# Where the lengths of the keys are computed in a second-order attention: on the transposed keys, or with tokens on partitions

## The chip, the core and the metric

The kernel runs on one core of one Trainium2 chip. A core has five engines with an instruction queue each: TensorE (PE in the profile; PEld is its loader of weights), VectorE (DVE), ScalarE (ACT), GpSimd (POOL) and SyncE (SP), and 16 DMA engines. Each queue is worked off in order, and an instruction starts when the semaphores that it waits for have been reached. The metric is the time of one execution on the device in microseconds, as the median of the runs shown.

## What is computed

The program is a graph network of two layers for 3125 nodes, 256 channels and 100,000 edges. Each layer adds to `x` a graph attention over the edges, a "mix" attention over all nodes, and a feed-forward part. The change touches the mix of layer 1, which has 8 heads of 32 channels (`N` = 3125, `scale` = 32 to the power 1/4):

```python
def _normalize(t):
    n = jnp.linalg.norm(t, axis=-1, keepdims=True)
    return t / jnp.maximum(n, EPS)
...
v1 = jnp.concatenate([jnp.ones((B, H, N, 1), dtype=v.dtype), v], axis=-1)
qn = _normalize(q) * (scale * temperature)
kn = _normalize(k) * scale
vN = v1 / N
kv_mod = jnp.einsum('bhni,bhnj,bhne->bhije', kn, kn, vN)
kv = jnp.einsum('bhnd,bhne->bhde', kn, vN)
vsum = jnp.sum(vN, axis=-2)[:, :, None, :]
y = A * jnp.einsum('bhni,bhnj,bhije->bhne', qn, qn, kv_mod) + scale ** 2 * Bc * jnp.einsum('bhnd,bhde->bhne', qn, kv) + scale ** 4 * Cc * vsum
```

So each key is divided by its length over the 32 channels of its head and multiplied by `scale`; then sums over all tokens of products of two key channels and a value channel are needed, and sums of one key channel and a value channel.

## The kernel before, in words

**Layer 1.** Two recorded streams of work share the engines. The graph attention (`l1_gnn_slots`, `by_slots`) goes through 25 blocks of 128 nodes, in 63 steps of up to 16 edges per node. GpSimd gathers a row of keys and values for each edge slot (L635) into one of five `kv` buffers. TensorE turns the edge features (L2596), ScalarE copies them out (L2598), TensorE multiplies them by the weights (L2599) into one of two `e` buffers in PSUM, and VectorE adds them to the gathered rows (L2604). VectorE then multiplies by the query (L985), sums over the channels (L989), and weights and halves the values (L1014, L1020); TensorE adds up what is left (L1023), which frees `kv` for the next gathers.

**The mix beside it.** `l1_mix_pairs` is a Python generator. After each of the 63 steps, `Beside` takes about two of its units, so that its instructions are recorded between those of the graph attention. A scheduler then fixes the order on each engine; the order of recording sets priorities, not the order itself. For each half of the heads (`c` = 0, 1; four heads, 128 channels) there is a key pass over all tokens and then a query pass. The key pass goes by groups of 4 tiles of 125 tokens (6 groups of 500 tokens and one of 125).

**For a group** `unit_T` computes the transposed keys, channels on partitions and tokens along the free dimension: TensorE multiplies (L2879), ScalarE adds the bias into `x` (L2884) and squares it (L2888), TensorE sums the squares over each head's 32 partitions with the block-diagonal matrix of ones `k.bd`, which also spreads each sum over the 32 partitions (L2890), ScalarE takes the root (L2892), VectorE clamps it (L2893), takes the reciprocal (L2894) and multiplies `x` by it and by `scale` (L2895). All of these are 128 x 500. The query pass uses the same function.

**For a tile** of 125 tokens: TensorE computes the values (L2912) into bank 0 of the two-bank PSUM tile `w`, of which there is one buffer; VectorE sets a column of ones (L2920) and adds the bias (L2921); TensorE turns the keys (L2924) into bank 1; ScalarE copies them out (L2925) and squares them (L2926); TensorE adds the tile to the moments `mom` (L2927, L2930, L2933). For the products of two different channels, TensorE multiplies the transposed keys of each head by `sel`, which has two ones in each column, so that each column is a sum of two channels (L2944, two heads in the two banks of `w`); ScalarE squares both banks in one instruction (L2949); after two such rounds TensorE multiplies the squares by the values and adds to `pairs` (L2953). The constants `neg` and `selT` later take the squares of single channels off again.

Of the kernel before, what the change touches and what calls it, by code (L numbers as in the profile page):

```python
# [10 lines left out]
F32 = mybir.dt.float32  # L11
I32 = mybir.dt.int32
BF16 = mybir.dt.bfloat16
AF = mybir.ActivationFunctionType
ALU = mybir.AluOpType
# [4 lines left out]
P = 125  # L20
# [39 lines left out]
def load_w(k, pool, w, name):  # L60

    kk, m = w.shape
    t = pool.tile([128, kk // 128, m], F32, name=name, tag=name)
    k.nc.sync.dma_start(t, w.rearrange("(c p) m -> p c m", p=128))
    return t


def load_col(k, pool, b, name):

    m = b.shape[0]  # L70
    t = pool.tile([128, m // 128], F32, name=name, tag=name)
    k.nc.sync.dma_start(t, b.rearrange("(c p) -> p c", p=128))
    return t
# [217 lines left out]
def after(k, ins, others):  # L291

    for other in others:
        k.tc.add_manual_dep(
            ins.ins, other.ins.name,
            mybir.DependencyInfo(mybir.DependencyClass.Sync, mybir.DependencyReason.DATA),
            reason="rows of the table",
        )
# [2543 lines left out]
def l1_mix_pairs(k, tabs, a, pl):  # L2842
# [6 lines left out]
    nc, NT, N = k.nc, k.NT, k.N  # L2849
    s = 32.0 ** 0.25  # L2850
    one, wp, xp, sp, ip, pp, pa, pb = pl
    two = lambda: pp.tile([128, 2, 512], F32, name="w", tag="w")
    ps_tile = lambda: two()[:, 0]
    wqkv = load_w(k, one, a["Wqkv"], "wqkv")
    bcol = load_col(k, one, a["bqkv"], "bcol")
# [6 lines left out]
    for h in range(8):  # L2862
        r = slice(h % 4 * 32, h % 4 * 32 + 32)
# [5 lines left out]
    def load_cols(gi, ng):  # L2869
        xT = ip.tile([128, 2, 4 * P], F32, name="xTg", tag="xTg")  # L2870
        nc.sync.dma_start(xT[:, :, : ng * P], tabs.cols[gi, :, :, : ng * P])
        return xT

    def unit_T(xT, ch, ng, scale, factor):

        w_ = ng * P
        ps = ps_tile()
        for ci in range(2):
            nc.tensor.matmul(  # L2879
                ps[:, :w_], wqkv[:, ci, ch * 128 : ch * 128 + 128],  # L2880
                xT[:, ci, :w_], start=(ci == 0), stop=(ci == 1),
            )
        x = wp.tile([128, 4 * P], F32, name="x", tag="x")
        nc.scalar.activation(  # L2884
            x[:, :w_], ps[:, :w_], AF.Identity, bias=bcol[:, ch : ch + 1], scale=scale
        )
        sq = xp.tile([128, 4 * P], F32, name="xsq", tag="xsq")
        nc.scalar.activation(sq[:, :w_], x[:, :w_], AF.Square)  # L2888
        ps = ps_tile()
        nc.tensor.matmul(ps[:, :w_], k.bd, sq[:, :w_], start=True, stop=True)  # L2890
        r = xp.tile([128, 4 * P], F32, name="r", tag="r")
        nc.scalar.activation(r[:, :w_], ps[:, :w_], AF.Sqrt)  # L2892
        nc.vector.tensor_scalar_max(r[:, :w_], r[:, :w_], 1e-12)  # L2893
        nc.vector.reciprocal(r[:, :w_], r[:, :w_])  # L2894
        nc.vector.scalar_tensor_tensor(  # L2895
            x[:, :w_], x[:, :w_], factor, r[:, :w_], op0=ALU.mult, op1=ALU.mult
        )
        return x

    for c in range(2):  # L2900
        pairs = pa.tile([128, 512], F32, name="pairs", tag="pairs")
        mom = pb.tile([128, 512], F32, name="mom", tag="mom")
        for gi, (g0, ng) in enumerate(k.groups):
            xT = load_cols(gi, ng)
            kT = unit_T(xT, 2 + c, ng, 1.0, s)
            for j in range(ng):
                i = g0 + j
                first, last = i == 0, i == NT - 1
                tk = slice(j * P, j * P + P)
                ps = two()  # L2910
                for ci in range(2):
                    nc.tensor.matmul(  # L2912
                        ps[:P, 0, :128], xT[:, ci, tk],
                        wqkv[:, ci, 2 * D + c * 128 : 2 * D + c * 128 + 128],
                        start=(ci == 0), stop=(ci == 1),
                    )
                kv = wp.tile([P, 257], F32, name="kvt", tag="kvt")
                k2 = wp.tile([P, 128], F32, name="k2", tag="k2")
                v = kv[:, 128:256]
                nc.vector.memset(kv[:, 256:], 1.0)  # L2920
                nc.vector.tensor_tensor(  # L2921
                    v, ps[:P, 0, :128], bv[:, c * 128 : c * 128 + 128], op=ALU.add
                )
                nc.tensor.transpose(ps[:P, 1, :128], kT[:, tk], k.ident)  # L2924
                nc.scalar.copy(kv[:, :128], ps[:P, 1, :128])  # L2925
                nc.scalar.activation(k2, ps[:P, 1, :128], AF.Square)  # L2926
                m0 = nc.tensor.matmul(  # L2927
                    mom[:, :257], kv[:, :128], kv, start=first, stop=last, skip_group_check=True
                )
                m1 = nc.tensor.matmul(  # L2930
                    mom[:, 257:385], k2, v, start=False, stop=last, skip_group_check=True
                )
                m2 = nc.tensor.matmul(  # L2933
                    mom[:, 385:386], v, k.ones_col[:P], start=False, stop=last, skip_group_check=True
                )
                if first:
                    after(k, m1, [m0])
                    after(k, m2, [m0])
                sqs = []
                for h0 in (0, 2):  # L2940
                    ps = two()
                    for b in range(2):
                        rows = slice((h0 + b) * 32, (h0 + b) * 32 + 32)
                        nc.tensor.matmul(  # L2944
                            ps[:P, b, :496], kT[rows, tk], sel[rows], start=True, stop=True,
                            tile_position=((h0 + b) * 32, 0),
                        )
                    sq = sp.tile([128, 2, 4 * P], F32, name="sq", tag="sq")
                    nc.scalar.activation(sq[:P, :, :496], ps[:P, :, :496], AF.Square)  # L2949
                    sqs += [sq[:, 0], sq[:, 1]]  # L2950
                for h in range(4):
                    rows = slice(h * 32, h * 32 + 32)
                    nc.tensor.matmul(  # L2953
                        pairs[rows, :496], v[:, rows], sqs[h][:P, :496], start=first, stop=last,
                        skip_group_check=True, tile_position=(0, h * 32),
                    )
                yield
# [16 lines left out]
        for t in range(4):  # L2974
            f = min(128, 496 - t * 128)
            fs = slice(t * 128, t * 128 + f)
            ps = ps_tile()
# [8 lines left out]
        ps = ps_tile()  # L2986
# [10 lines left out]
        for h in range(4):  # L2997
# [3 lines left out]
                op0=ALU.mult, op1=ALU.subtract,  # L3001
            )
        for gi, (g0, ng) in enumerate(k.groups):
            w_ = ng * P
            qT = unit_T(load_cols(gi, ng), c, ng, s, temp[:, c : c + 1])
            x = ip.tile([P, 4, D], F32, name="xg4", tag="xg4")
# [3 lines left out]
            ps = ps_tile()  # L3010
# [5 lines left out]
            ps = ps_tile()  # L3016
# [13 lines left out]
            for t in range(4):  # L3030
                f = min(128, 496 - t * 128)
                sqs = []
                for h0 in (0, 2):
                    ps = two()
                    for b in range(2):
# [3 lines left out]
                            start=True, stop=True, tile_position=((h0 + b) * 32, 0),  # L3039
                        )  # L3040
                    sq = sp.tile([128, 2, 4 * P], F32, name="sq", tag="sq")
# [14 lines left out]
            for j in range(ng):  # L3056
                ps = ps_tile()
# [158 lines left out]
def layer1(k, dram, a, out, tabs, order, show):  # L3216
    sub = lambda pre: {s[len(pre) :]: v for s, v in a.items() if s.startswith(pre)}
    top = ExitStack()
    (wp,) = pools(k, top, [("d_w", 1)])
    weights = l1_ffn_weights(k, wp, sub("L1_ffn_"))  # L3220
    with ExitStack() as st:
        units = l1_mix_pairs(k, tabs, sub("L1_mix_"), l1_mix_pools(k, st))
        beside = Beside(units, 2 * k.NT + 12 * len(k.groups), sum(len(steps(n)) for n in SLOTS))
        gout, sent = l1_gnn_slots(k, dram, tabs, order, a["edge_attr_64"], sub("L1_gnn_"), beside)
        beside.rest()
    with top as st:
        xp, wp = pools(k, st, [("x3", 1), ("r_wk", 4)])
        x = xp.tile([P, k.NT, D], F32, name="x3")
        for g0, ng in k.groups:
            k.nc.sync.dma_start(x[:, g0 : g0 + ng], tok(tabs.x)[:, g0 : g0 + ng])  # L3230

        def bring(g0, ng):
            g = slice(g0, g0 + ng)
            part = wp.tile([P, 4, D], F32, name="part", tag="part")
            after(k, k.nc.sync.dma_start(part[:, :ng], tok(gout[0 : k.N, :])[:, g]), sent)
            k.nc.vector.tensor_tensor(x[:, g], x[:, g], part[:, :ng], op=ALU.add)

        l1_ffn(k, dram, x, sub("L1_ffn_"), out, weights, bring)
# [111 lines left out]
```

## Time and profile before

| What | Value |
|---|---|
| Median of 3 runs | 5826.44 us (5819.25 to 5837.37) |
| The profiled execution | 5829.55 us, span 5827.8 us |
| TensorE busy (weight loads) | 4671.1 us, 80% of the span (2785.9) |
| VectorE busy | 4216.7 us, 72% |
| ScalarE busy | 1582.9 us, 27% |
| GpSimd busy | 2901.4 us, 50% |
| Layer 1's graph attention (first and last L2599) | 3504.6 to 5555.4 us |
| L2884, one of 500 tokens | 677 ns |
| L2921, one of 125 x 128 | 283 ns |
| L2925, L2926 | 266 and 283 ns |
| L2944, idle time of the squares' engine behind it | 186.0 us, 97 times |

"Busy" is the time in which an engine worked on an instruction. A busy TensorE is not TensorE at its peak, as matmuls overlap and its clock is granted in parts. A row of a group reads: line, engine, operation, output and inputs, shapes, count, then busy us and mean ns of one, then the idle time of the engine just before these instructions and the instruction whose end released most of it. Each matmul of 32-bit numbers is two instructions in the trace. Some records of matmuls are missing, so that counts can be below those of the program. The mean of one is from one profiled execution, that of the table.

### The profile page before, as it was taken

What the parts mean: (1) busy time and instruction counts of PE and PEld (TensorE: products, weight loads), DVE (VectorE), ACT (ScalarE), POOL (GpSimd) and SP (SyncE); (2) the same over time, 40 slices, a digit from 0 to 9 for tenths busy, and PEclk for the clock granted to TensorE, in tenths of its full rate; (3) what the DMA queues carried; (4) which work ended last, traced back from release to release, by engine and by line L of the source; (5) the groups of instructions that cost most, each with busy time, mean ns of one, the idle gap of its engine ahead of it and who ended that gap; (6) DMA issues with size and microseconds to landing.
All of it is one profiled execution on the core that took longest, in us unless ns stands there. A gap on an engine that the chain in (4) does not pass through costs nothing. (4 is left out here: it accounts for less than half of the span.)

```text
span 5827.8 us, 50130 instructions
## 1 busy us (share of the span) xinstructions
PE 4671.1 (80%) x16621; PEld 2785.9 (48%) x16621; DVE 4216.7 (72%) x6090; ACT 1582.9 (27%) x3284; POOL 2901.4 (50%) x2945
## 2 busy tenths in 40 slices
PE   3467997799957998789858857789888888888778
PEld 1245775566535676556545523334333434333335
DVE  5188888888578888988631256668787778878847
ACT  1033233233323334333411102222222222222221
POOL 2475775577366775667541035344444444444411
PEclk8778998799978999899859977888898789989979
DMA  5266776677466776667454355444453444545410
GB/s 152 61 197 187 217 198 187 182 210 207 146 178 192 208 207 188 198 195 208 147 164 137 109 167 173 121 124 129 137 148 119 132 124 139 150 131 150 137 59 23
DMA packets 374285, 908.58 MB, mean 156 GB/s; under 512 B 94268, under 2 KB 170074, under 8 KB 373892
## 3 DMA queue, kind: packets, MB, share of 16 engines
q0 software_dynamic: 232624, 725.48, 43.1%
q1 hardware_dynamic: 137412, 168.23, 8.9%
q10 hardware_dynamic: 3982, 11.59, 0.5%
q8 instruction: 134, 2.20, 0.2%
q14 instruction: 133, 1.09, 0.1%
HBM read 813.62 MB, written 91.30 MB: 155 GB/s over the span
## 5 line engine op out<-in xcount | busy, mean ns | idle before, releaser
L635 POOL DMA_INDIRECT kv<-kvtab,slots x2499 | 2425.6, 971 | 1742.1 <-PE acc L1023 691.6
L1170 PE MATMUL cps<-kv,ident 128*128 128x256 f32 x2644 | 688.8, 415 | 64.4 <-DVE kv L1154 63.1
L2604 DVE TENSOR_TENSOR kv<-kv,e 128x1024 f32<-128x1024 f32 (+1 forms) x448 | 503.4, 1137 | 252.1 <-PE e L2599 226.1
L1170 PEld LDWEIGHTS cps<-kv,ident 128*128 128x128 f32 x2644 | 548.9, 211 | 214.3 <-DVE kv L1154 82.4
L2599 PE MATMUL e<-weT,eaT 128*128 128x512 f32 (+1 forms) x896 | 516.6, 673 | 66.4 <-ACT eaT L2598 64.7
L1114 DVE TENSOR_TENSOR kv<-kv,qa 128x1792 f32<-128x1792 f32 (+2 forms) x230 | 478.6, 2081 | 98.4 <-DMA kv<-kvtab,slots 85.5
L1117 DVE TENSOR_REDUCE al<-kv 128x28 f32<-128x1792 f32 (+2 forms) x230 | 479.4, 2084 | 7.9
L1154 DVE TENSOR_TENSOR kv<-kv,qa 128x1792 f32<-128x1792 f32 (+2 forms) x230 | 475.3, 2074 | 0.0
L1857 PE MATMUL mm<-hTm,w 128*128 128x500 f32 (+1 forms) x896 | 364.4, 551 | 30.5 <-DVE xcur L1883 21.7
L1875 PE MATMUL mm<-w,hid 128*125 128x256 f32 x1600 | 378.5, 385 | 1.8 <-ACT hid L1865 1.8
L1023 PE MATMUL acc<-kv,ident 128*128 128x256 f32 x896 | 268.3, 463 | 76.9 <-DVE kv L1020 72.0
L1875 PEld LDWEIGHTS mm<-w,hid 128*125 128x125 f32 x1600 | 296.4, 190 | 65.2 <-issue 19.6
L2599 PEld LDWEIGHTS e<-weT,eaT 128*128 128x128 f32 (+1 forms) x896 | 153.7, 207 | 286.9 <-ACT eaT L2598 146.9
L1023 PEld LDWEIGHTS acc<-kv,ident 128*128 128x128 f32 x896 | 206.7, 237 | 165.8 <-DVE kv L1020 107.9
L1857 PEld LDWEIGHTS mm<-hTm,w 128*128 128x128 f32 x896 | 162.3, 196 | 177.5 <-issue 130.9
L989 DVE TENSOR_REDUCE al<-kv 128x56 f32<-128x1792 f32 (+2 forms) x115 | 238.7, 2075 | 4.6 <-issue 3.7
L985 DVE TENSOR_TENSOR kv<-kv,qa 128x1792 f32<-128x1792 f32 (+2 forms) x115 | 238.8, 2077 | 1.3
L1014 DVE TENSOR_TENSOR kv<-kv,al 128x1792 f32<-128x1792 f32 (+2 forms) x115 | 235.0, 2080 | 0.0
L2598 ACT COPY eaT<-e 128x128 f32<-128x128 f32 (+1 forms) x448 | 109.5, 267 | 411.7 <-PE e L2596 411.2
L1547 PE MATMUL mm<-ident,xh 125*128 125x125 f32 x400 | 96.7, 336 | 136.3 <-ACT xh L1537 128.0
L140 PE MATMUL mm<-wqv,hTm 128*125 128x512 f32 x400 | 187.5, 607 | 7.4 <-DMA wqv<-in_L_mix_Wv_dram 6.3
L1865 ACT ACTIVATE hid<-mm,b 128x500 f32<-128x500 f32 (+1 forms) x224 | 133.8, 632 | 198.3 <-PE mm L1857 196.8
(414 smaller groups left out, 7693.1 us busy)
## 6 DMA issues: line engine op xcount, KB each, us to landing
kv<-kvtab,slots POOLq DMA_INDIRECT x2499, 3.7
w<-in_L_ffn_w_dram SPq DMA_DIRECT2D x32, 512.0 KB
qd<-qT SPq DMA_DIRECT2D x24, 500.0 KB
kvtab<-st SPq DMA_DIRECT2D x12, 1000.0 KB
qT<-qd SPq DMA_DIRECT2D x24, 500.0 KB
xTg<-xcols SPq DMA_DIRECT2D x24, 500.0 KB
w<-in_L_mix_W_dram SPq DMA_DIRECT2D x8, 1024.0 KB
xs<-zero SPq DMA_DIRECT2D x16, 512.0 KB
```

Of the source, the lines that this page charges most:

```text
L635: return k.nc.gpsimd.indirect_dma_start(out=out, out_offset=None, in_=table, in_offset=bass.IndirectOffsetOnAxis(ap=index, axis=0),)
L985: nc.vector.tensor_tensor(kv[:, :m, :D], kv[:, :m, :D], q.unsqueeze(1).to_broadcast([128, m, D]), op=ALU.mult,)
L989: nc.vector.tensor_reduce(al[:, b0 : b0 + m], hv(kv[:, :m, :D]), axis=AX.X, op=ALU.add)
L1023: nc.tensor.matmul(acc[:, :D], k.ident, kv[:, j, D:], start=(b0 + j == 0), stop=(kv is bufs[-1][2] and j == left[-1]),)
L1114: nc.vector.tensor_tensor(kv[:, :m, :D], kv[:, :m, :D], q.unsqueeze(1).to_broadcast([128, m, D]), op=ALU.mult)
L1117: nc.vector.tensor_reduce(t["al"][:, b0 : b0 + m], self.heads(kv[:, :m, :D]), axis=AX.X, op=ALU.add)
L1154: nc.vector.tensor_tensor(v, v, t["w"][:, b0 : b0 + m].unsqueeze(3).to_broadcast([128, m, H, D // H]), op=ALU.mult)
L1170: self.k.nc.tensor.matmul(t["acc"][:, :D], self.k.ident, kv[:, j, D:], start=(b0 + j == 0), stop=(b == len(t["subs"]) - 1 and j == left[-1]),)
L1857: nc.tensor.matmul(ps[:, :w_], W["w1"][:, c, j * 128 : j * 128 + 128], o["hT"][:, c, :w_], start=(c == 0), stop=(c == 1),)
L1875: nc.tensor.matmul(ps[:P, :D], s["hid"][:, c, j * P : j * P + P], W["w2"][:, c, :], start=(c == 0), stop=False,)
L2599: nc.tensor.matmul(e[:, :n].rearrange("p b d -> p (b d)"), eaT[r], weT[r, :n].rearrange("p b d -> p (b d)"), start=True, stop=True,)
L2604: nc.vector.tensor_tensor(t, t, e[:, :n].unsqueeze(2).to_broadcast([128, n, 2, D]), op=ALU.add)
```

## The change

For the keys, `unit_T` is replaced by a new function. It stops after the squares: `x` stays as it is, without its length. The squares of a tile of 125 tokens become the stationary operand, and four columns of `k.bd` the moving one, so that the sums come out with tokens on partitions and one column for each head: 125 x 4 for a tile, 125 x 16 for a group. Root, clamp and reciprocal work on these. The factor is then put on in two places: VectorE multiplies the turned keys by it as it copies them out of PSUM, in place of ScalarE's copy, and ScalarE takes it as the scale operand when it squares the sums of two channels, one head in each instruction. The square `k2` is taken from the scaled keys in SBUF. The queries keep `unit_T`.

```diff
+    head0 = k.bd.rearrange("p (h d) -> p h d", d=32)[:, :, 0]
+
+    def keys_T(xT, ch, ng):
+
+        w_ = ng * P
+        ps = ps_tile()
+        for ci in range(2):
+            nc.tensor.matmul(
+                ps[:, :w_], wqkv[:, ci, ch * 128 : ch * 128 + 128],
+                xT[:, ci, :w_], start=(ci == 0), stop=(ci == 1),
+            )
+        x = wp.tile([128, 4 * P], F32, name="x", tag="x")
+        nc.scalar.activation(
+            x[:, :w_], ps[:, :w_], AF.Identity, bias=bcol[:, ch : ch + 1], scale=1.0
+        )
+        sq = xp.tile([128, 4 * P], F32, name="xsq", tag="xsq")
+        nc.scalar.activation(sq[:, :w_], x[:, :w_], AF.Square)
+        ps = ps_tile()
+        for j in range(ng):
+            nc.tensor.matmul(
+                ps[:P, j * 4 : j * 4 + 4], sq[:, j * P : j * P + P], head0, start=True, stop=True
+            )
+        r = wp.tile([P, 16], F32, name="r4", tag="r4")
+        nc.scalar.activation(r[:, : ng * 4], ps[:P, : ng * 4], AF.Sqrt)
+        nc.vector.tensor_scalar(
+            r[:, : ng * 4], r[:, : ng * 4], 1e-12, 1.0 / s, op0=ALU.max, op1=ALU.mult
+        )
+        nc.vector.reciprocal(r[:, : ng * 4], r[:, : ng * 4])
+        return x, r
...
-            kT = unit_T(xT, 2 + c, ng, 1.0, s)
+            kT, r4 = keys_T(xT, 2 + c, ng)
...
-                nc.scalar.copy(kv[:, :128], ps[:P, 1, :128])
-                nc.scalar.activation(k2, ps[:P, 1, :128], AF.Square)
+                rj = r4[:, j * 4 : j * 4 + 4]
+                nc.vector.tensor_tensor(
+                    kv[:, :128].rearrange("p (h d) -> p h d", d=32),
+                    ps[:P, 1, :128].rearrange("p (h d) -> p h d", d=32),
+                    rj.unsqueeze(2).to_broadcast([P, 4, 32]), op=ALU.mult,
+                )
+                nc.scalar.activation(k2, kv[:, :128], AF.Square)
...
-                    nc.scalar.activation(sq[:P, :, :496], ps[:P, :, :496], AF.Square)
+                    for b in range(2):
+                        nc.scalar.activation(
+                            sq[:P, b, :496], ps[:P, b, :496], AF.Square,
+                            scale=rj[:, h0 + b : h0 + b + 1],
+                        )
```

In the new kernel the lines that the prediction names are L2907 (was L2879, for the keys), L2919 (the lengths), L2951 (was L2921), L2954 (L2924), L2956 (the new multiplication), L2961 (L2926), L2962 (L2927), L2979 (L2944), L2985 (the squares, L2949) and L2992 (L2953).

## The prediction

> **What bounds the kernel now.** I read the page's totals first (TensorE is busy for 80% of the span, VectorE for 72%, and neither is full), then found the two stretches in which the changed code runs: the first and last instructions of the sum-of-pairs matmuls (L2953) and of the key pass's `x` (L2884) put the key pass of the first half of the heads at 3513 to 3995 us and that of the second at 4565 to 4991 us. The view of busy time by stretch gives for them:
>
> ```profile
> 3513.00:3995.00 482.00, 393.90 (x1271) 182.18 (x1271) 341.56 (x356) 119.98 (x266) 217.31 (x225) 0.84 0.46 133
> 4565.00:4991.00 426.00, 374.32 (x1253) 172.64 (x1253) 321.54 (x351) 121.15 (x264) 189.51 (x192) 0.87 0.44 129
> ```
>
> Columns: stretch, its length, busy us of TensorE, weight loads, VectorE, ScalarE, GpSimd, then granted clock, DMA share, GB/s. TensorE leaves 88 + 52 = 140 us idle in the two passes, VectorE 245, ScalarE 667. So TensorE is nearest to the bound, and the passes end when its stalls end. Next, what TensorE waited for: the groups of the two instructions that stand right behind the keys' normalisation. First the timeline at one normalisation:
>
> ```profile
> 3703.59 0.41 DVE L2893 TENSOR_SCALAR r<-r 128x500 f32<-128x500 f32 x1
> 3704.11 3.27 DVE L2894 RECIPROCAL r<-r 128x500 f32<-128x500 f32 x1
> 3707.48 0.67 DVE L2895 SCALAR_TENSOR_TENSOR x<-x,r 128x500 f32<-128x500 f32 x1
> 3708.26 0.28 DVE L2921 TENSOR_TENSOR kvt<-w,bv 125x128 f32<-125x128 f32 x1
> 3708.60 0.37 PE L2924 MATMUL w<-ident,x 128*125 128x128 f32 x1 [0.85 <-DVE kvt L2921]
> ```
>
> The reader is to see that the keys' transpose (L2924) stands behind 4.35 us of VectorE work, of which the reciprocal is three quarters. In three such stretches VectorE is full, TensorE is not, and its granted clock is low (same columns):
>
> ```profile
> 3619.00:3629.00 10.00, 4.12 (x15) 2.68 (x15) 10.00 (x12) 2.57 (x6) 2.17 (x3) 0.70 0.39 130
> 3701.50:3711.50 10.00, 8.14 (x24) 4.46 (x24) 9.97 (x13) 1.01 (x4) 0.00 (x0) 0.66 0.00 0
> 3776.50:3786.50 10.00, 5.17 (x15) 3.15 (x15) 10.00 (x15) 2.77 (x7) 0.00 (x0) 0.67 0.01 2
> ```
>
> The instructions of L2924 and of the squares (L2949), each line's own view, give the totals over both passes:
>
> ```profile
> L2924 PE MATMUL w<-ident,x x50: 272/273/577, 3545.1 to 4973.2; 128*125 128x128 f32 x50
> ...
>   DVE kvt L2921: 34.9, 21
>   DVE x L2895: 20.0, 9
> ```
>
> ```profile
> L2949 ACT ACTIVATE sq<-w 125x992 f32<-125x992 f32 x100 | 99.7, 997 | 186.0 <-PE w L2944 186.0
> L2944 PE MATMUL w<-sel,x 32*125 32x496 f32 x400 | 137.9, 749 | 13.4 <-ACT sq L2949 13.3
> ```
>
> Of the 54.9 us at L2924, 22.0 is idle time of the matmuls themselves (13.8 behind L2921, 8.2 behind L2895, from the view of who was waited for); the rest is the weight loader's, which overlaps. The 12 waits behind that 22.0 are as many as there are groups of 500 tokens in the two passes. The 13.3 us at L2944 is the wait for the squares, since the `w` tile has one buffer.
>
> **What the Trainium skill says.** "VectorE: DVE Perf Modes", the walkthrough of the pipeline: a reciprocal is an iterative divide that repeats 8 times. The trace agrees that it is dear: 3.27 us for 500 columns against 0.67 for a multiplication of the same width (L2895). "ScalarE: Activation LUTs", what a table load costs: 186 ns + 0.833 ns per column, and 93 ns more for each 128x1 operand. The trace agrees: 992 columns without one took 997 ns (formula 1012), 500 columns with a bias operand (L2884) 677 ns (695). "TensorE: Matmul & The Clock Gate", Part 1: after a window of some 3.4 us without work the array runs at half clock. The three stretches above, with stalls of 4 to 6 us, agree.
>
> **The change, part by part.**
> 1. *Removed on VectorE*: in 12 full and 2 short groups L2893, L2894, L2895: 12 x (0.41 + 3.27 + 0.67) + 2 x 1.4 = 55.0 us. *Added*: 14 x (a clamp-and-scale and a reciprocal of 125x16; the nearest rows, 128x8, take 0.23 and 0.19) = 6 us, of which little shows; 50 multiplications of 125x128 out of PSUM (L2956 in the new kernel), each like L2921, 0.28: 14. Net -35 us of 663.
> 2. *The transposes no longer wait for the norm.* `x` is ready as ScalarE writes it. Gain: the 22.0 us. The low clock in the three stretches goes too: 17.4 us of matmul at 0.68 would take 14.1 at the pass's 0.84: 3 us.
> 3. *The rest of VectorE's queue moves up.* TensorE's other waits for VectorE are 40.4 us in the first pass (L1023 19.3, L2596 16.6, L961 4.5) and 19.9 in the second (7.6 and 12.3). VectorE's load falls by 35/663 = 5%, but its longest blocks go. I take a quarter, 15 us; bounds 0 and 30. A check: in the query pass after 4991, where the same reciprocals remain and the chain can be followed, L2894 has 2.9% of 569 us = 16.5 of its 20.5 us on the chain, 80%. 80% of 55 is 44; my sum of points 2 and 3 is 22 + 3 + 15 = 40.
> 4. *Squares split and given a scale operand.* 100 of 0.997 become 200 of 496 columns. L2884's 677 ns at 500 gives 0.674 each: 135 us, +35 of ScalarE, and the pair takes about 1.3 in place of 1.0. ScalarE is idle 73% of the time, so its load costs nothing; what costs is that `w` is held. In the new order of TensorE I priced what stands between the first and second pair of L2944 (L2979 after) by its means in the timeline (two passes of L2599 1.15, L2596 0.3, L2953 0.26) and counted as stall what is missing to the squares' time plus 0.15 for the handing over. For before this gives 13.9 us in 21 tiles (the trace: 13.3 in 20). For after, with 1.3: 25.0 in 48. The same for the sums of pairs behind the second pair: 1.8 before, 5.5 after. Cost: 11 + 4 = 15; bounds 0 (if matmul clock fills it) and 25.
> 5. *The moments (L2927) now wait for VectorE in place of ScalarE.* ScalarE's copy cost TensorE 9.6 us of waiting. In the new order of VectorE an L985 or L989 (2.0 to 2.3 us) stands between the v add and the new multiplication in 24 of 50 tiles, a whole value stage in 3. Behind the multiplication stand L2604, which frees the edge buffers that TensorE fills, and L985. Most of these tiles have the 8 matmuls of L1023 or two L2599 in front of the moments, so the scheduler covers the wait; 6 tiles have nothing between. I take +3; bounds -5 and +50 (1 us for each tile). The square `k2` now reads SBUF and follows the multiplication; it comes ahead of L2930, not of `w`'s release: nothing.
> 6. *The lengths on TensorE.* Removed: 28 passes of L2890, 24 of 0.6 and 4 of 0.27 = 15 us busy. Added: 100 passes of 4 columns; the nearest row, L2933 with one column, 0.22, overlapping by half: 11 to 22. I take +2; bounds -4 and +7.
> 7. *ScalarE's other edits*: 50 copies of 0.27 go, the root shrinks from 0.59 to about 0.25; hidden, as ScalarE waits for TensorE (186 us at L2949 alone). The programs hold 27 table loads for the root before and after. No transfer is added. The orders on GpSimd and SP only shift within the passes, and the order in the query passes comes out nearly the same.
>
> Sum: -40 + 15 + 3 + 2 = -20 us. The profiled execution took 5829.55 (span 5827.8), so 5809.5; the median of before, 5826.44, lies 3.1 lower: 5806.
>
> **Rivals.** A difference under 0.3% (17.5 us) is what a measurement of this kernel can't tell from none.
> - *The squares and the tight TensorE take it all.* TensorE is 88% busy in the second pass; there only 5.7 us of the 22 lie, and only 52 us are idle at all. If point 3 gives nothing: -25 + 20 = -5: 5821. For it: TensorE's share. Against it: the 80% of the chain.
> - *The moments become VectorE's prisoners.* One mechanism: L2956 stands in VectorE's queue behind 2 us operations and itself waits for a transpose, so that both engines stop for each other in every tile. At 1 us for each of 50 tiles: -40 + 17 + 50 = +27: 5853. It decides from (40 - 17)/50 = 0.46 us a tile on. For it: VectorE already waits for TensorE (45.9 us at L2604 in the second pass). Against: the filler in the new order.
> - *More goes than the waits show.* If the reciprocals also held GpSimd's gathers and the edge loads (VectorE sat 47 us at L2587 for edge data in the first pass), the full 55 could go with little given back: 5778. Against: those waits end by a DMA, which nothing here makes faster.
>
> **How the numbers follow.** Forecast -20: 0.48, within it 0.36 beyond the 0.3% and 0.12 inside. First rival 0.19 (0.14 inside, 0.05 slower). Second 0.22 (0.20 slower, 0.02 inside). Third 0.11, faster. So faster 0.47, within 0.28, slower 0.25. The likeliest one's own range is 5792 to 5822. For eight in ten I go from 5778, the third rival, to 5838, half-way into the second; that leaves out about half of the second and part of the third.
>
> **What would show it.** Right: no L2894 in the key passes and TensorE's wait at the transpose below 5 us; VectorE's busy time lower by about 35; the squares at 0.67 each, with a wait at L2979 of 20 to 30 us. Wrong: a wait of TensorE for the new multiplication at the moments over 20 us in total, or VectorE waiting over 20 us for the transposes; a pass of the second half no shorter than 426 us; or squares at 0.58, which would halve point 4.

## The result and the profile after

The changed kernel takes 5796.19 us (median of 5 runs, 5794.36 to 5798.5), the kernel before 5826.44 us beside it (5 runs, 5817.17 to 5837.37). The ratio is 0.9947, with a 95% interval from 0.9931 to 0.9963: 31 us less (22 to 40). The profiled execution took 5798.5 us with a span of 5796.7; the span before was 5827.8.

The page's totals of the kernel after, busy time and share of the span by engine:

```profile
PE 4669.3 (81%) x16693; PEld 2773.6 (48%) x16693; DVE 4178.2 (72%) x6126; ACT 1595.8 (28%) x3334; POOL 2902.5 (50%) x2945
```

VectorE did 38.5 us less (4216.7 before), which is the sum of the prediction's step 1. TensorE did as much as before (4671.1), although its granted clock rose from 0.871 to 0.885 over the span: something that the prediction doesn't have keeps it busy for longer. The two key passes, in the view of busy time by stretch, with the columns of the prediction's first fence:

```profile
3518.00:3986.00 468.00, 408.52 (x1322) 181.45 (x1322) 334.17 (x391) 128.43 (x298) 230.23 (x238) 0.92 0.50 145
4536.00:4959.00 423.00, 374.46 (x1287) 166.81 (x1285) 300.17 (x372) 126.51 (x290) 189.56 (x194) 0.96 0.46 133
```

TensorE's idle time in the passes fell from 140 to 59 + 49 = 108 us, and its clock in them went from 0.84 to 0.92 and from 0.87 to 0.96. The first pass is 14 us shorter, the second 3. So it isn't two equal shares: measured on ScalarE's 63 copies that end the steps of the graph attention (L1027), and with both first L2599 laid on one another, the kernel after is ahead by 44 us near the end of the first pass, by 22 at it, by 29 to 36 in the query pass after it, by 53 within the second key pass and by 31 at its end. The graph attention runs ahead while keys are processed, and part of that is given back towards the end of each key pass. Of the 31 us at the end of the second pass 29 were there before it began, so that pass adds almost nothing that lasts.

A normalisation now, VectorE's timeline (start, length, engine, line):

```profile
3704.08 2.02 DVE L985 TENSOR_TENSOR kv<-kv,qa 128x1792 f32<-128x1792 f32 x1
3706.02 0.17 DVE L2924 TENSOR_SCALAR r<-r 125x16 f32<-125x16 f32 x1
3706.10 0.28 DVE L2951 TENSOR_TENSOR kvt<-w,bv 125x128 f32<-125x128 f32 x1
3706.30 2.01 DVE L989 TENSOR_REDUCE al<-kv 128x56 f32<-128x1792 f32 x1
3708.22 0.24 DVE L2927 RECIPROCAL r<-r 125x16 f32<-125x16 f32 x1
...
3710.60 0.29 DVE L2956 TENSOR_TENSOR kvt<-w,r 125x128 f32<-125x128 f32 x1 [1.98 <-PE w L2954]
```

The 4.35 us of before are two instructions of 0.17 and 0.24, and the v add (the bias onto the values, L2951) stands between them. The last line is the new wait: VectorE sat 1.98 us until TensorE had turned the keys; TensorE's timeline has matmuls of L2599, L961 and L962 from 3707.53 on, and the transpose behind them at 3710.19. What the transpose waits for, its own line's view:

```profile
L2954 PE MATMUL w<-ident,x x50: 272/273/575, 3530.7 to 4944.1; 128*125 128x128 f32 x50
...
  DVE kvt L2951: 21.0, 18
```

The 20.0 us behind the normalised `x` are gone, the 34.9 behind the v add are 21.0, of which 7.1 are the matmuls' own (22.0 before).

The time that doesn't come back lies on TensorE, in the groups of the sums of pairs. Before:

```profile
L2953 PE MATMUL pairs<-sq,kvt 125*32 125x496 f32 x400 | 111.3, 679 | 8.1 <-ACT sq L2949 8.1
```

After:

```profile
L2992 PE MATMUL pairs<-sq,kvt 125*32 125x496 f32 x400 | 192.6, 609 | 14.1 <-ACT sq L2985 14.0
L2979 PE MATMUL w<-sel,x 32*125 32x496 f32 x400 | 115.2, 653 | 0.0
```

The same 400 instructions, each even a little shorter (609 ns for 679), keep TensorE busy for 81 us more, while idle time behind the squares is small: 14.0 us here, none at L2979. The timelines show why. TensorE before, at the end of a tile:

```profile
3761.20 1.10 PE L2944 MATMUL w<-sel,x 32*125 32x496 f32 x4
3762.22 1.03 PE L2953 MATMUL pairs<-sq,kvt 125*32 125x496 f32 x4
3763.18 0.44 PE L2596 MATMUL e<-ident,ea 128*128 128x128 f32 x2
3763.55 1.03 PE L2953 MATMUL pairs<-sq,kvt 125*32 125x496 f32 x4
```

and after:

```profile
3713.90 1.02 PE L2992 MATMUL pairs<-sq,kvt 125*32 125x496 f32 x2
3714.85 1.10 PE L2979 MATMUL w<-sel,x 32*125 32x496 f32 x4
3715.88 1.02 PE L2992 MATMUL pairs<-sq,kvt 125*32 125x496 f32 x2
```

A matmul is two instructions. Before, the matmuls of two heads (x4) took 1.03 us together; after, one head's (x2) takes 1.02 alone. Two heads use different columns of the array (`tile_position=(0, h * 32)`) and ran side by side: one square made both heads' data ready at once, and their matmuls stood next to one another. With a square for each head, the order on TensorE puts other work between them: of the stretches of this line in the trace, 84 of 92 held two matmuls before and the other 8 four, while after, 159 of 179 hold one alone. That matmuls at different tile positions can run at the same time is what the Trainium skill, "TensorE: Matmul & The Clock Gate", Part 3 on packing small matmuls, states; the two timelines agree.

### The profile page after: what moved, and what is told of

Read it like the earlier page. It is cut to its first block, busy times and chain, and to the rows that moved or that the text cites. A ratio compares the mean times of both kernels' runs of the same rounds, so it can differ in the third digit from the quotient of the medians.

```text
span 5796.7 us, 50370 instructions
## 1 busy us (share of the span) xinstructions
PE 4669.3 (81%) x16693; PEld 2773.6 (48%) x16693; DVE 4178.2 (72%) x6126; ACT 1595.8 (28%) x3334; POOL 2902.5 (50%) x2945
## 5 line engine op out<-in xcount | busy, mean ns | idle before, releaser
L2604 DVE TENSOR_TENSOR kv<-kv,e 128x1024 f32<-128x1024 f32 (+1 forms) x448 | 504.8, 1139 | 243.7 <-PE e L2599 212.7
L2599 PE MATMUL e<-weT,eaT 128*128 128x512 f32 (+1 forms) x896 | 492.0, 645 | 63.5 <-ACT eaT L2598 61.5
L1023 PE MATMUL acc<-kv,ident 128*128 128x256 f32 x896 | 251.4, 440 | 86.8 <-DVE kv L1020 81.8
L2599 PEld LDWEIGHTS e<-weT,eaT 128*128 128x128 f32 (+1 forms) x896 | 149.3, 202 | 263.0 <-ACT eaT L2598 139.7
L1023 PEld LDWEIGHTS acc<-kv,ident 128*128 128x128 f32 x896 | 194.5, 223 | 158.2 <-DVE kv L1020 109.6
L2992 PE MATMUL pairs<-sq,kvt 125*32 125x496 f32 x400 | 192.6, 609 | 14.1 <-ACT sq L2985 14.0
```

The lines of the kernel that those rows point to most:

```text
L1023: nc.tensor.matmul(acc[:, :D], k.ident, kv[:, j, D:], start=(b0 + j == 0), stop=(kv is bufs[-1][2] and j == left[-1]),)
L2599: nc.tensor.matmul(e[:, :n].rearrange("p b d -> p (b d)"), eaT[r], weT[r, :n].rearrange("p b d -> p (b d)"), start=True, stop=True,)
L2604: nc.vector.tensor_tensor(t, t, e[:, :n].unsqueeze(2).to_broadcast([128, n, 2, D]), op=ALU.add)
L2992: nc.tensor.matmul(pairs[rows, :496], v[:, rows], sqs[h][:P, :496], start=first, stop=last, skip_group_check=True, tile_position=(0, h * 32),)
```

## The experiments

Two theories at the start. *The wait*: the transposes waited for the norm, and that wait is what went (the prediction's step 2). *The queue*: what counts is the time that VectorE's in-order queue holds, whoever waits for its result; behind the reciprocal stand the v add and L2604, which frees the edge buffers. Beside these, the price of each of the two places where the factor is put on. All ratios are to the kernel before on the same chip; us are the ratio's distance from 1 times 5828.

**e1: the keys' reciprocal replaced in the kernel before.** The keys are not divided by their lengths.

```diff
-        nc.vector.reciprocal(r[:, :w_], r[:, :w_])
+        if ch < 2:
+            nc.vector.reciprocal(r[:, :w_], r[:, :w_])
+        else:
+            nc.vector.tensor_scalar_mul(r[:, :w_], r[:, :w_], 1.0)
```

> The kernel before, with the keys' reciprocal (L2894, key passes alone) replaced by a multiplication by 1.0 of the same 128x500, so the keys' lengths are not inverted; the queries keep theirs. This takes 12 x (3.27 - 0.41) + 2 x 0.7 = 36 us from VectorE and leaves every instruction and every wait where it is recorded. Theory A (VectorE's long block ahead of the transposes is what the change takes away): 36 of the 55 us go, so 36/55 of the 40 us of gross gain, with nothing given back: -26 us, about 5800. Theory B (the gain comes from the scheduler's new order, or from a part other than the norm): within 8 us of before, 5818 to 5834.

0.9933 (0.9910 to 0.9957): -39 us (25 to 52) for 36 us of VectorE work (12 x (3.27 - 0.41) + 2 x (0.94 - 0.22)). So the reciprocals of the keys cost about their full length in the kernel before, though the matmuls of the transposes had waited for only 22 us.

**e2: the dependence of the transposes taken away in the kernel before.** The normalised keys go into `r`, and transposes and sums read `x` without its length; VectorE does all its work.

```diff
-            x[:, :w_], x[:, :w_], factor, r[:, :w_], op0=ALU.mult, op1=ALU.mult
+            (x if ch < 2 else r)[:, :w_], x[:, :w_], factor, r[:, :w_], op0=ALU.mult, op1=ALU.mult
```

> The kernel before, with the keys' normalised product written to r instead of x, so that the transposes and the sums of pairs take the keys without their factor. VectorE does all the work of before; only TensorE's wait for it is gone. Theory A1 (it is the wait of the transposes that costs): the 22 us of idle time at L2924 and 3 us of low clock go: -25 us, about 5801. Theory A2 (it is the time in VectorE's queue, since the v add and L2604 stand behind the norm anyway): within 8 us of before.

1.0018 (1.0009 to 1.0028): 10 us slower. What the transposes (L2924) wait for in it:

```profile
L2924 PE MATMUL w<-ident,x x50: 272/273/577, 3544.3 to 4967.8; 128*125 128x128 f32 x50
...
  DVE kvt L2921: 41.0, 20
```

The wait for `x` is gone and the wait for the v add has grown from 34.9 to 41.0: the v add stands in VectorE's queue behind the same reciprocal, so TensorE is mostly released by another name. Of the matmuls' own 22.0 us, 16.3 are still there. So e2 shows that the dependence of the transposes on the normalised `x` is worth nothing; what it would be worth to be rid of the waiting, e2 can't say. Nor was it followed why the kernel got slower.

**e5: the reciprocals given back to the kernel after, with nobody waiting for them.**

```diff
         nc.scalar.activation(r[:, : ng * 4], ps[:P, : ng * 4], AF.Sqrt)
+        rd_ = xp.tile([128, 4 * P], F32, name="r", tag="r")
+        nc.vector.reciprocal(rd_[:, :w_], x[:, :w_])
```

> The changed kernel, with a reciprocal of 128x500 (of the keys, into a tile that nobody reads) recorded behind the root in each group of the key passes: VectorE gets 12 x 3.27 + 2 x 0.93 = 41 us back, and nothing waits for it but what stands behind it in VectorE's queue. Theory A2 (the queue's time is what costs, as e2 said): most of the gain over before is lost, 5820 to 5840. Theory A1 (the wait of the transposes for the factor): no later than 5804.

1.0024 (1.0009 to 1.0039) against before, so 1.0024/0.9947 = 1.0077 against the kernel after: 45 us lost for 41 us of work (12 x 3.27 + 2 x 0.94). The timeline of all engines in e5, four lines of it:

```profile
3704.04 3.28 DVE L2925 RECIPROCAL r<-x 128x500 f32<-128x500 f32 x1 [0.94 <-ACT x L2912]
...
3707.23 1.75 DVE L2604 TENSOR_TENSOR kv<-kv,e 128x1024 f32<-128x1024 f32 x2
...
3708.45 0.69 PE L925 MATMUL e<-ident,xg 128*128 128x128 f32 x2 [1.39 <-DVE kv L2604]
...
3708.98 0.28 DVE L2953 TENSOR_TENSOR kvt<-w,bv 125x128 f32<-125x128 f32 x1
```

No instruction reads what the reciprocal writes, and in its line's view nobody waits for it. But L2604 starts only when it ends, and TensorE's next matmul into an edge buffer sits 1.39 us until L2604 has freed that buffer. The matmuls' wait at the transposes rose by only 4.8 us (7.1 to 11.9), so that 40 of the 45 us (32 to 58) were lost elsewhere. Not all of it is the reciprocal's length: the queue also stood for 15.7 us in front of it, until ScalarE had written `x`. With e1 and e2 this decides between the two: time in VectorE's queue costs, without anybody waiting for the result, and the dependence on the result doesn't.

**e4, e6 and e12: the factor's two places taken out of the kernel after, one at a time and together.** e4 squares both banks at once and so leaves the factor off the products of channels; e6 lets ScalarE copy the turned keys and leaves it off the moments; e12 does both.

```diff
-                    for b in range(2):
-                        nc.scalar.activation(
-                            sq[:P, b, :496], ps[:P, b, :496], AF.Square,
-                            scale=rj[:, h0 + b : h0 + b + 1],
-                        )
+                    nc.scalar.activation(sq[:P, :, :496], ps[:P, :, :496], AF.Square)
```

```diff
-                nc.vector.tensor_tensor(
-                    kv[:, :128].rearrange("p (h d) -> p h d", d=32),
-                    ps[:P, 1, :128].rearrange("p (h d) -> p h d", d=32),
-                    rj.unsqueeze(2).to_broadcast([P, 4, 32]), op=ALU.mult,
-                )
-                nc.scalar.activation(k2, kv[:, :128], AF.Square)
+                nc.scalar.copy(kv[:, :128], ps[:P, 1, :128])
+                nc.scalar.activation(k2, ps[:P, 1, :128], AF.Square)
```

> The changed kernel, with the squares in one instruction for two banks again and no scale operand, so that the products of pairs are left without the keys' factor. By the working of the prediction the 15 us that the split costs come back: about 5781 (before: 5826, changed: 5796). Rival, that the split costs nothing: 5793 to 5799.

> The changed kernel, with the turned keys copied and squared by ScalarE out of PSUM as before, so that the moments are left without the keys' factor; the squares of pairs keep it. This takes the new multiplication (L2956, 50 x 0.28 = 14 us) and the two steps through VectorE's queue in each tile away. By the working of the prediction it gives back 3 us: 5790 to 5797. Rival (the moments are held up by VectorE, which the other gains hide): 15 us or more, 5781 or lower.

> The changed kernel with joint squares (as e4) and ScalarE's copy of the turned keys (as e6), so that the keys' factor is computed and put on nowhere: the gross gain of the change without its two costs. If the two costs (18 us each) are independent: 5796 - 18 - 18 = 5760. If both are one and the same wait (w held longer): 5775. The 40 us of gross gain in the prediction would give 5786.

| Kernel | Ratio to before (95%) | us | VectorE busy against 4216.7 |
|---|---|---|---|
| after | 0.9947 (0.9931 to 0.9963) | -31 | -38.5 |
| e4, joint squares | 0.9917 (0.9891 to 0.9942) | -48 | -34.9 |
| e6, copy on ScalarE | 0.9919 (0.9894 to 0.9945) | -47 | -44.5 |
| e12, both | 0.9884 (0.9862 to 0.9906) | -68 | -45.4 |

The split squares cost 17 us (after against e4) and 21 (e6 against e12); the multiplication on VectorE costs 16 (after against e6) and 20 (e4 against e12). By the intervals one such difference is uncertain by about its own size, and the mean of two, 19 and 18 us, still by some 13. The costs add, as far as these intervals tell; the 5775 us that one and the same wait would have given lie just outside e12's (a ratio of 0.9912). And the whole gain, with neither put on, is 68 us and not the prediction's 40.

What the split takes is TensorE's time. The sums of pairs in e4:

```profile
L2988 PE MATMUL pairs<-sq,kvt 125*32 125x496 f32 x400 | 117.5, 681 | 0.0
```

and in e6, where squares stay split:

```profile
L2988 PE MATMUL pairs<-sq,kvt 125*32 125x496 f32 x400 | 187.4, 604 | 8.5 <-ACT sq L2981 8.3
```

In all the kernels here, wherever both banks are squared at once the line takes 106 to 118 us, wherever they are split 187 to 206. Of these some 75 us (192.6 - 117.5 and 187.4 - 112.4 for e12) only a quarter reaches the end. TensorE's whole busy time is up by no more than 35 and 49 us (4634.4 to 4669.3, and 4624.3 to 4673.6), as other matmuls got shorter (L2979 takes 115.2 us after and 125.0 in e4) and its clock is higher with the split (in the key passes 0.92 and 0.96, against 0.87 and 0.94 in e4); the rest must lie in time in which it stood idle.

**e3: the squares alone split in the kernel before**, with a scale operand of ones.

```diff
-                    nc.scalar.activation(sq[:P, :, :496], ps[:P, :, :496], AF.Square)
+                    for b in range(2):
+                        nc.scalar.activation(
+                            sq[:P, b, :496], ps[:P, b, :496], AF.Square, scale=k.ones_col[:P]
+                        )
```

> The kernel before, with each square of two banks (L2949) split into two instructions of one bank with a scale operand of ones: the split of the change by itself. By the working of the prediction the pair takes 1.3 in place of 1.0 us and w is held longer: +15 us, about 5841, with TensorE's wait for squares up from 13 to 25 us at L2944. Rival: ScalarE is idle 73% of the time and the scheduler fills in: within 6 us of before.

1.0070 (1.0047 to 1.0092): +41 us, twice what the split costs in the kernel after. The sums of pairs and the transposes in it:

```profile
L2956 PE MATMUL pairs<-sq,kvt 125*32 125x496 f32 x400 | 203.4, 646 | 14.2 <-ACT sq L2950 14.2
...
L2924 PE MATMUL w<-ident,x 128*125 128x128 f32 x50 | 16.6, 332 | 39.3 <-DVE kvt L2921 19.7 <-DVE x L2895 19.6
```

TensorE has 92 us more of sums of pairs, and its wait at the transposes grew from 22.0 to 39.3 in the new order; the longer wait for the squares that was expected at L2944 did not come (0.0 us of the matmuls', 13.3 before).

Where the longer sums of pairs reach the end can be read on VectorE. For each tile it fills the column of ones in one of two `kvt` buffers, and it may do so only when the sums of pairs of the tile before last have read the values there. So its queue stands until they have. From the views of the sums of pairs, who waited for them, in the kernel before:

```profile
  DVE kvt L2920: 38.6, 11
```

and in e3:

```profile
  DVE kvt L2920: 74.0, 21
```

That is 35 us more, of the 41 lost. The same wait (L2950) is 20.8 us in e4 and 40.8 in the kernel after, 22.7 in e12 and 33.2 in e6: 20 and 10 us more with the split, for 17 and 21 lost. So the split, too, seems to cost through VectorE's queue, and much of why it costs more in e3 shows here. But no run takes this wait away by itself, and e14 below warns against counting it one for one.

**e11 and e14: what a new order alone does.** In the kernel before, two instructions of a tile are recorded in the other order: in e11 ScalarE's square of the turned keys ahead of its copy, in e14 the column of ones after the v add.

```diff
-                nc.scalar.copy(kv[:, :128], ps[:P, 1, :128])
                 nc.scalar.activation(k2, ps[:P, 1, :128], AF.Square)
+                nc.scalar.copy(kv[:, :128], ps[:P, 1, :128])
```

```diff
-                nc.vector.memset(kv[:, 256:], 1.0)
                 nc.vector.tensor_tensor(
                     v, ps[:P, 0, :128], bv[:, c * 128 : c * 128 + 128], op=ALU.add
                 )
+                nc.vector.memset(kv[:, 256:], 1.0)
```

> The kernel before with the square of the turned keys (L2926) recorded ahead of their copy (L2925): the same instructions and sizes, but the scheduler gives TensorE another order in the key passes. A control for what a new order alone is worth. If the differences of the other runs are those of the work: within 10 us of before. If a new order alone gives 20 us or more either way, the terms of this study under that size mean little.

> The kernel before with the memset of the column of ones recorded behind the v add in place of ahead of it: TensorE's order hardly changes, VectorE's memsets stand elsewhere. Second control: within 5 us of before.

e14: 0.9989 (0.9976 to 1.0003), so -14 to +2 us, no difference that can be told, although VectorE's idle time at the column of ones and the v add together fell from 54.7 to 25.3 us. e11: 1.0033 (1.0021 to 1.0045), 19 us slower (12 to 26), just under the 20 that its expectation names. It is no clean control: the copy that the moments wait for can come later by the square's 0.28 us in each of 50 tiles, up to 14 us, and VectorE's wait for the sums of pairs (L2920) is 53.2 us in it against 38.6. So an order can move the time by as much as the split or the multiplication costs. That each of the two was found in two pairs of kernels speaks for them; that the order has no part in them is not shown. The 45 us of e5 and the 68 of e12 are well beyond this, and terms of a few us (the prediction's TensorE lengths, +2) can't be told apart by such runs.

**e9, e13 and e10: a version without either cost.** The lengths are taken token by token as in the change, but the reciprocal is spread over the 32 channels by ScalarE, turned back by TensorE against the identity, and multiplied into `x` while still in PSUM. So the keys are divided where they were before, with no split square and no multiplication for each tile; and the same function can serve the queries.

```diff
-        nc.tensor.matmul(ps[:, :w_], k.bd, sq[:, :w_], start=True, stop=True)
-        r = xp.tile([128, 4 * P], F32, name="r", tag="r")
...
+        rb = xp.tile([P, 16, 32], F32, name="rb", tag="rb")
+        nc.scalar.copy(
+            rb[:, : ng * 4], r[:, : ng * 4].unsqueeze(2).to_broadcast([P, ng * 4, 32])
+        )
+        ps = ps_tile()
+        for j in range(ng):
+            nc.tensor.matmul(
+                ps[:, j * P : j * P + P],
+                rb[:, j * 4 : j * 4 + 4].rearrange("p h d -> p (h d)"), k.ident[:P, :P],
+                start=True, stop=True,
+            )
         nc.vector.scalar_tensor_tensor(
-            x[:, :w_], x[:, :w_], factor, r[:, :w_], op0=ALU.mult, op1=ALU.mult
+            x[:, :w_], x[:, :w_], factor, ps[:, :w_], op0=ALU.mult, op1=ALU.mult
         )
```

e9 does this for keys and queries, e13 for the keys alone, e10 as e9 and likewise for the denominators of the query pass.

> A version meant to beat both: the kernel before, where unit_T (keys and queries) takes lengths with tokens on partitions as the change does, inverts 125x16, ScalarE spreads each number over 32 columns, and TensorE turns it back to channels on partitions against the identity; the product with x is one VectorE instruction of 128x500 out of PSUM. Joint squares and ScalarE's copy of the turned keys stay. VectorE per group: about 1.1 in place of 4.35 us, in key and query passes. If VectorE's time is what counts (A2): the keys give about what e1 gave, 40, and the queries, where the reciprocal was on the chain for 80% of its time, up to 30 more, less 10 for the longer way round: 5760 to 5780. Rival: the way through TensorE, ScalarE, VectorE, ScalarE and TensorE again, with one buffer of w held in turn, costs what it saves: no better than the changed kernel, 5796 or more.

> As e9, but for the keys alone; the queries keep the reciprocal of 128x500. Tells what the keys' part of e9's 77 us is. By e1 (36 us less on VectorE: -41) and with 45 us less on VectorE here: -45 to -50, about 5780, and the queries' part about 30. Rival: the scheduler's order in the key passes is what gives, and the queries' part is under 10: 5762 or lower.

> As e9, and the second reciprocal of the query pass (the denominators u, 128x500) goes the same way: 12 x 3.7 us less on VectorE, 4 + 4 more small matmuls and two more ScalarE copies in a group. If VectorE's time is what counts: 15 to 30 us less than e9. Rival: here the denominators are needed only at the end of the group (z), so the reciprocal was hidden: within 8 us of e9.

e9: 0.9874 (0.9848 to 0.9899), 5751.61 us: 73 us under the kernel before (77 by the medians, which is the figure in e13's expectation) and faster than the kernel after. e13: 0.9915 (0.9890 to 0.9940), -50 us. So the queries bring the other 23, give or take 21. Most of it doesn't lie in the query passes: from the last sum of pairs of the second key pass to the last L2599 the profiled executions take 562 us in e13 and 567 in e9, while the sums of pairs of the second key pass, whose code is the same in both, span 398 and 378. VectorE's timeline in e9 at a normalisation:

```profile
3700.82 0.17 DVE L2898 TENSOR_SCALAR rq<-rq 125x16 f32<-125x16 f32 x1
...
3702.21 0.25 DVE L2899 RECIPROCAL rq<-rq 125x16 f32<-125x16 f32 x1
...
3705.06 0.68 DVE L2911 SCALAR_TENSOR_TENSOR x<-x,w 128x500 f32<-128x500 f32 x1 [0.28 <-PE w L2906]
```

The way from the clamp to the normalised keys is no shorter (4.9 us here, 4.6 before), but VectorE is held for 1.1 us of it in place of 4.35, and L2604 runs in between. That fits the theory of the queue once more: the latency stayed, the queue time went, and the gain is larger than the change's. e10: 0.9882 (0.9853 to 0.9911), no better than e9, although VectorE is busy for another 43 us less (4097.7 against 4140.8). So not every microsecond taken from the queue counts; its expectation's rival, that the denominators are needed only at the end of a group, fits, but why was not followed.

## Why the prediction was right, and where it was not

The forecast was 5806, measured were 5796: -20 foreseen, -31 found, inside the likeliest case's own range (5792 to 5822). The gain and the costs were both too small, and the place where the gain lies and the way in which the split costs were not foreseen. That the sum came near is in good part luck.

1. *VectorE's work, -35.* Right: -38.5 by the page's totals.
2. *The transposes no longer wait for the norm, -22.* The reading fell. The waits shrank (22.0 to 7.1 for the matmuls, where below 5 was to show the forecast right), but e2 takes away the dependence that they were put down to and gains nothing, and e1 gains more than all of them. The clock did rise, but not only for want of stalls: without the split (e4) it came to 0.87 and 0.94 (448 and 408 us), and the rest to 0.92 and 0.96 came with the split's extra work.
3. *The rest of the queue, -15.* Here lay nearly everything. Points 2 and 3 stood at 40 together; e12 gives 68 (55 to 80). The prediction had a second estimate at hand, the chain's 80% of 55 = 44; it too was low. In the kernels without the split, time saved stands to VectorE time saved (by the pages' totals) as 39 to 32 in e1, 50 to 38 in e13, 48 to 35 in e4, 68 to 45 in e12 and 73 to 76 in e9: 1.0 to 1.5 us for each. Against e9, e10 is the exception, with none for 43.
4. *The squares, +15.* The size was right (17 and 21), the mechanism not. The prediction priced stalls: 25.0 us at L2979 and 5.5 at the sums of pairs. The matmuls' stalls came out at 0.0 and 14.0, no more in all than the 21 before, and the wait of 20 to 30 us at L2979 that was to show the forecast right did not come. What the split takes is the side-by-side run of two heads' matmuls, 81 us more busy time at L2992, of which about a quarter reaches the end, it seems by VectorE's wait for these sums (20.8 us in e4, 40.8 after). No run splits the squares and keeps the two heads' matmuls together, so that the squares' own time and the longer hold of `w` are not ruled out as a part of it. The squares' own duration, 0.674 foreseen, is 0.668.
5. *The moments, +3.* This is the term that was mis-sized the most on the cost side: 16 and 20. The wait that the prediction feared is small, 8.2 us of TensorE's at L2962, against 9.6 for ScalarE's copy before. L2956's own view, first what it waited for, then who waited for it:

```profile
L2956 DVE TENSOR_TENSOR kvt<-w,r x50: 273/283/293, 3531.9 to 4944.6; 125x128 f32<-125x128 f32 x50
...
  PE w L2954: 9.1, 10
...
  PE mom L2962: 8.2, 16
```

   What is left is queue time: 50 x 0.283 = 14 us, and 9.1 us in which VectorE itself waits for the transpose with all behind it. At 1.0 to 1.5 us for each us of the queue, the 14 alone make 14 to 21; this fits, but was not tried by itself. One more wait comes with the multiplication: the matmuls' wait for the v add at the transposes is 7.1 us after and 7.0 in e4, but 0.3 in e6 and 0.4 in e12, where ScalarE copies. The prediction had the 14 us in its step 1, but gave them no price of their own.
6. *TensorE's lengths, +2, and ScalarE's edits, 0.* Not separable: they are below what a reordering may move.

The sum by the runs: -68 + 19 + 18 = -31. The prediction's -40 + 15 + 3 + 2 = -20 came near because the gain was too small by 28 and the costs by 17. The first rival (all taken by the squares and a tight TensorE) has the right engine, but e12 shows the gain far above its 25. The second named L2956 and foresaw the wait, which at 9.1 us in 10 of 50 tiles stayed below its 0.46 us a tile, as does the whole cost of 18 us (0.36 a tile). The third, that more goes than the waits show, holds for the gross gain (68 against its 55), but not with little given back; its own mechanism, the gathers, was not tried. Two readings in the prediction are off, without weight for its sum: VectorE's wait at L2604 in the second pass is 51.2 us and not 45.9, and TensorE's stalls in the three stretches are 3.7 to 5.2 us and not 4 to 6.

Still open: how much of the difference between the split's 41 us in the kernel before and its 19 in the kernel after is VectorE's wait for the sums of pairs, how much the wait at the transposes, and how much the order; what a VectorE microsecond is worth in the query passes; and why the second key pass is only 3 us shorter although TensorE's clock rose as much there.

## What to carry to other kernels

Where one engine's in-order queue feeds all the others, price an edit by the time it adds to or takes from that queue, not only by the wait that the profile puts beside the edited instruction: when the dependence alone is taken away, the wait moves to the next name in the queue. To test it, take the dependence away without the work, and put the work back without the dependence. One price does not hold everywhere: e10 took 43 us of denominators off the same queue for nothing. Before splitting an instruction in two, look at what its single completion let run side by side. Count the busy time of the followers, and look at who waits for them to end: this cost need not show in a wait at the edited instruction.

## What the runs showed of the hardware

- A reciprocal of 125 x 16 takes 0.244 us, of 128 x 500 3.27: with tokens on partitions, and without the 32-fold spread, the same 2000 lengths (500 tokens, four heads) cost a thirteenth.
- Two matmuls of 32 columns each and 496 moving columns, at different columns of the array and next to one another in the queue, take 1.03 us together, and one of them takes 1.02 alone.
- TensorE's mean granted clock in the two key passes was 0.84 and 0.87 before (82% and 88% busy), 0.92 and 0.96 after (87% and 89%), 0.93 and 1.00 in e6 (89% and 92%, in 3518 to 3968 and 4520 to 4925). It is higher with the split squares, but the busy share alone doesn't give it: e4, at 86% and 87%, has 0.87 and 0.94 (in 3518 to 3966 and 4520 to 4928). That the clock pays for part of the split's extra work fits this, but was not tried by itself.
